# Giving each of five queues its own lead in a written-out instruction order: a four-layer graph network on one Trainium2 core

## The chip, the cores and the metric

The kernel runs as one program on one core of a Trainium2 chip. A core has five engines with a queue each: TensorE (PE) for matrix products, VectorE (DVE), ScalarE (ACT), GpSimd (POOL), and SyncE (SP), which only issues transfers. An engine works through its queue in order; between engines there are semaphores. The metric is the device time of one execution in microseconds (us), lower is better. The profile is one profiled execution of the same program.

## The reference

There are B = 32 independent batches of N = 512 nodes with D = 128 features, and a 512 x 512 adjacency matrix of zeros and ones with about 16 neighbours per node. Four layers follow one another, each as `x = x + layer(relu(layernorm(x)), adj)`:

```python
# layer 0: the largest value over the neighbours
p, q = h @ (W1 - W2), h @ W2
out = max over j of relu(p[i] + q[j] + b) * adj[i, j]
# layer 1: four steps, with earlier results concatenated (1, 1, 2, 3 inputs)
upd = concat(l2norm(adj, 2) @ (f @ ws + bs), f @ wn + bn, l2norm(adj, 1).T @ (f @ wd + bd))
f = tanh(upd @ wu + bu)
# layer 2
out = (adj / rowsum) @ (h @ weight) + bias
# layer 3: four steps of a gated recurrent unit
m = adj.T @ (h @ weight[i])
r, z = sigmoid(...), sigmoid(...); n = tanh(xn + r * hn); h = (1 - z) * n + z * h
```

All weights are shared by the batches.

## The kernel before, in words

`gnn_stack` calls `fast`, which computes all batches, then a flag that says whether any batch needs the slow path `general` (none does in these inputs). In `fast` a batch is 21 parts in a row:

- *prepare* (function `prepare`): load x and adj (1 MB, ACT's DMA queue), layer norm, transposes of adj (`pat`) into `at`, the products q and p (`pq`, then `qn`, `pn` on DVE), a table of q in DRAM (`qtab`, SP's queue).
- *counts*: prefix counts of each adjacency row as matmuls (`pc`), cast on ACT (`cc`) and spread by four SP transfers each (`ccd`).
- *keys*: degrees on POOL, the matmuls `pkey`, the largest eight of a row on DVE (`top`), from which indices of neighbours come (`idx`).
- *rows* and *gather0* to *gather3* (function `gathers`): 28 indirect transfers of table rows (`G`, POOL's queue), each taken into a running maximum `gm` on DVE; beside it one-hot matrices `oh` (DVE, some on ACT), matmuls `pa`, and their running maximum `acc` on DVE, 32 per batch, eight in each of the four gather parts.
- *first*: both maxima are joined to x1; adj is loaded again as `an` (POOL's queue).
- *layer1* and *layer10* to *layer13* (function `layer1`): each step transposes its input (`pf`), splits it into two fp32r parts (`hi` on ACT, `lo` on DVE), multiplies both by `at` and `an` (`pg`, 16 matmuls), scales on DVE (`ag`), and adds up `pu`; tanh on ACT gives `f`.
- *layer2*, *layer3* (function `layer23`): layer 2 and the norm before layer 3 (`po`, `pt`).
- *layer30* to *layer33*: a GRU step each: `pg` (8 matmuls), copy `mT`, the gate products `pk`, sigmoids on ACT (`gate`), `phn` and `pxn`, `nn` and `h` on DVE and POOL, transposes `ph`, and again `hi` and `lo`.
- *out*: the last sum `xo` and the store.

The order of each queue isn't that of the program text. Class `Flow` records every operation with an estimated duration (`cost`), up to AHEAD = 6 batches at a time, and gives them out one by one: in `step` it looks for the engine that can start something first, and on that engine, among the operations that can start at that time, takes the one with the smallest due time. The due time is set in `close`: the place of the batch times PACE, less the longest remaining chain inside the batch, less a lead of the part:

```python
op.due = n * self.pace - op.due - op.lead
```

Places come from `FIRST` and `LAST` (the first and last batches moved against an even spacing of one), and for the three groups of weight preparation from `WEIGHTS`: `first` (layer 0's weights), `rest` (layer 1's), `last` (layers 2 and 3). Leads come from function `lead`: `LEADS` for all batches, with `LEADS0` added for the first and `LEADSN` for the last. Before the change a part has one lead for all five queues, set as `F.lead` at the start of the part and copied to each operation in `note`. Where its own timeline leaves PE idle for over 1 us, `clock` puts in small matmuls with no use of their result (`spin`), so that PE's clock stays up. Transfers are recorded like other operations, on the queue of the engine that issues them.

The line 529 of the profile is the helper that issues nearly every instruction, so the profile is read by the names of tiles.

Of the kernel before, what the change touches and what calls it, by code (L numbers as in the profile page):

```python
# [32 lines left out]
CODES = ((0, 1), (P, 1), (2 * P, 2), (4 * P, 4))  # L33
ONACT = (2, 2, 1, 0)
NLEFT = 7
PACE = 46.14
SPACING = 1.5
AHEAD = 6
BANKS = (1, 2, 2, 1)

LEADS = {
    "prepare": -28.3, "counts": -7.5, "keys": 16.5, "rows": 26.6,
    "gather0": 59.4, "gather1": 70.0, "gather2": 28.0, "gather3": 53.5,
    "first": 61.2, "layer1": 43.0, "layer10": 30.3, "layer11": 8.7,
    "layer12": 56.0, "layer13": -41.3, "layer2": 39.7, "layer3": 5.5,
    "layer30": 99.5, "layer31": 189.8, "layer32": 213.5, "layer33": 84.7,
    "out": 56.0,
}

LEADS0 = {  # L50
    "prepare": 18.5, "counts": 53.1, "keys": 4.8, "rows": -15.7,
    "gather0": 52.2, "gather1": 93.4, "gather2": -34.5, "gather3": -69.1,
    "first": 0.5, "layer1": 141.7, "layer10": 10.1, "layer11": 110.3,
    "layer12": -73.8, "layer13": -13.4, "layer2": 6.9, "layer3": 56.5,
    "layer30": 35.3, "layer31": 29.8, "layer32": 117.9, "layer33": 64.0,
    "out": 75.9,
}
LEADSN = {
    "prepare": -19.9, "counts": -18.3, "keys": -42.0, "rows": 46.6,
    "gather0": 15.9, "gather1": -47.7, "gather2": -77.8, "gather3": -4.3,  # L60
    "first": 13.3, "layer1": -33.7, "layer10": 14.0, "layer11": -36.5,
    "layer12": 103.7, "layer13": 62.6, "layer2": 212.2, "layer3": 99.8,
    "layer30": 182.6, "layer31": 105.8, "layer32": 85.0, "layer33": 161.6,
    "out": -15.2,
}
FIRST = (1.57, 0.36, -0.05, 0.0)
LAST = (0.0, 0.18, 0.33, 0.24, 0.3)
WEIGHTS = (-3.98, -2.44, -5.94)

LATE = {  # L70
    "xn2": ("xn0", 1), "hi2": ("qn", 1), "lo2": ("gm", 1), "mT": ("acc", 1), "hg": ("hT0", 1),
# [29 lines left out]
class View:  # L101


    def __init__(self, tile, shape, dtype, steps=(), lanes=None, region=None):
        self.tile, self.shape, self.dtype = tile, tuple(shape), dtype
        self.steps, self.lanes, self.region = steps, lanes or (0, shape[0]), region
# [196 lines left out]
class Flow:  # L303
# [9 lines left out]
    SPIN, IDLE = 0.23, 1.0  # L313
    WINDOW = 3.413
    EVENT = 0.13
    ENGINES = ("pe", "vec", "act", "pool", "sync")

    def __init__(self, nc, pace, ahead, slack=0.0):
        self.nc, self.pace, self.ahead, self.slack = nc, pace, ahead, slack
        self.rings, self.part, self.lanes = {}, [], {}  # L320
        self.lead = 0.0
        self.free = dict.fromkeys(self.ENGINES, 0.0)
        self.busy = dict.fromkeys(self.ENGINES, 0.0)
        self.spin, self.window, self.active, self.rate = None, 0, 0.0, 1.0
        self.gathered, self.port, self.turn, self.queue = 0.0, 0.0, 0, {}
        self.seen = {e: {} for e in self.ENGINES}
        self.waiting = {e: [] for e in self.ENGINES}
        self.vec = Engine(self, "vec", nc.vector)
        self.act = Engine(self, "act", nc.scalar)
        self.pool = Engine(self, "pool", nc.gpsimd)  # L330
        self.sync = Engine(self, "sync", nc.sync)
# [49 lines left out]

    def note(self, engine, fn, args, kw, outs, ins, cost, after):
        op = Op(engine, fn, args, kw, cost, after)
        op.lead = self.lead
        seen = set()
        for writes, views in ((False, ins), (True, outs)):
            for v in views:
                if not isinstance(v, View):
                    continue
                buf = v.tile  # L390
                for u, seen_as, w in buf.uses:
                    if u is op or not (writes or w) or not v.meets(seen_as):
                        continue
                    if id(u) not in seen:
                        seen.add(id(u))
                        op.before.append(u)
                if writes and buf.real is None and buf not in op.new:
                    op.new.append(buf)
                if writes and v.region is None and v.lanes == (0, buf.rows):
                    buf.uses = [c for c in buf.uses if c[0] is op]  # L400
                buf.uses.append((op, v, writes))
                if buf not in op.bufs:
                    op.bufs.append(buf)
                    buf.left += 1
        self.part.append(op)
# [75 lines left out]
    def step(self):  # L481
        best = None
        for e in self.ENGINES:
            now = [(t, op) for op in self.waiting[e] if (t := self.start(op)) is not None]
# [20 lines left out]
        if op.engine == "pe":  # L505
            t = self.clock(op, t)
        cost = op.cost + (self.EVENT * max(0, len(need) - 1) if op.engine != "pe" else 0.0)
        if op.engine == "pe":
# [350 lines left out]
def fast(ctx: ExitStack, tc: tile.TileContext, a: dict, out: bass.AP, bad):  # L859
# [10 lines left out]

    F = Flow(nc, PACE, AHEAD)
    F.share(ps, 8, {f"ps{s}": n for s, n in enumerate(BANKS)} | {"idle": 0})

    def lead(b, stage):
        own = LEADS0 if b == 0 else LEADSN if b == B - 1 else {}
        return LEADS[stage] + own[stage] if stage in own else LEADS[stage]

    def bank(s, shape, dtype, name):
        return F.tile(ps, shape, dtype, f"ps{s}", name, BANKS[s])
# [13 lines left out]
    for i in range(2):  # L893
# [3 lines left out]
            out=t[2 * P :, :].rearrange("(k p) d -> p k d", p=P),  # L897
# [82 lines left out]
    def prepare(b, xt, af):  # L980
# [60 lines left out]
        for t, (first, step) in enumerate(CODES):  # L1041
            F.sync.dma_start(
                out=tab[first : first + (P - 1) * step + 1 : step, :], in_=qn[:, t, :]
            )
        F.lead = lead(b, "counts")


        ccd = []
        for jt in range(NT):
# [10 lines left out]
            ccd.append(d)  # L1060

        F.lead = lead(b, "keys")


# [48 lines left out]
    def gathers(b, at, ccd, qhl, pn, tab, idx, has, dinv):  # L1113
# [15 lines left out]
        for jt in range(NT):  # L1129
            F.lead = lead(b, f"gather{jt}")  # L1130
            for k in range(1, KSLOT + 1):
                oh = F.tile(big, [P, 2, N], F32R, tag="oh", name=f"oh_{b}_{jt}_{k}", bufs=3)
                if k > KSLOT - ONACT[min(b, len(ONACT) - 1)]:

                    far = F.tile(big, [P, 2, N], BF16, tag="far", name=f"far_{b}_{jt}_{k}")
                    F.act.activation(far, ccd[jt], AF.Abs, bias=W.slot[:, k : k + 1])
                    F.act.activation(oh, far, AF.Relu, bias=W.ones[:, 0:1], scale=-1.0)
                else:
                    F.vec.tensor_scalar(oh, ccd[jt], NBASE + k, None, ALU.is_equal)
                for u in range(2):  # L1140
                    pa = pst(3, f"pa_{b}_{k}_{jt}_{u}")
                    F.mm(flat(pa), qhl[:, jt, u, :], oh[:, u, :], start=True, stop=True)
                    if k == 1 and jt == 0 and u == 0:
                        F.act.copy(acc, flat(pa))
                    else:
                        F.vec.tensor_max(acc, acc, flat(pa))
# [212 lines left out]
    def spin(n):  # L1359
# [5 lines left out]
    places = [  # L1365
        b - FIRST[min(b, len(FIRST) - 1)] - LAST[max(0, b - B + len(LAST) - 1)] for b in range(B)
    ]
    F.run(
        list(zip(WEIGHTS, (W.first, W.rest, W.last)))
        + [(p, partial(batch, b)) for b, p in enumerate(places)]  # L1370
# [471 lines left out]
```

## Time and profile before

| | us |
|---|---|
| median of 3 runs | 2907.83 (2904.98 to 2911.66) |
| span of the profiled execution | 2909.0 |
| TensorE busy | 2795.8 |
| TensorE's weight loads (beside it) | 1794.6 |
| VectorE busy | 2299.1 |
| ScalarE busy | 1268.4 |
| GpSimd busy | 1848.5 |

For the profiled execution only its span is given, from the first to the last instruction. In the profile a group is named by what it writes and reads ("pg<-at,lo" is a matmul into pg from at and lo). "[0.90 <-DVE lo L529]" behind a line says that the engine was idle for 0.90 us before it and that DVE's lo ended that. A row that begins with two times and a colon gives the busy time of each engine in that stretch of the span, with the number of its instructions. The clock is that which the chip granted to TensorE, 1.00 being full.

### The profile page before, as it was taken

The page shows a single profiled execution, that of the slowest core. Times are in us where ns is not written, and L with a number is a line of the kernel's source. Part 1 is how long each engine was busy: PE and PEld are TensorE (multiplying, and loading weights), DVE is VectorE, ACT ScalarE, POOL GpSimd, SP SyncE. Part 2 cuts the span into 40 slices and gives each one's busy share as a digit, 9 for nine tenths or more (in the row PEclk, how much of TensorE's full clock was granted, in tenths as well). Part 3 has the DMA queues.
Part 4 walks back from the last instruction along what each step waited for, and adds up shares of the span by engine and source line. Part 5 has one row for each costly group of instructions (what it writes and reads, how often), then busy time and mean ns, then how long its engine had stood idle before and what let it go on. Part 6 is the DMA issues. An engine that isn't in the chain of part 4 may idle for free.

```text
span 2909.0 us, 38588 instructions
## 1 busy us (share of the span) xinstructions
PE 2795.8 (96%) x11766; PEld 1794.6 (62%) x11766; DVE 2299.1 (79%) x5371; ACT 1268.4 (44%) x2622; POOL 1848.5 (64%) x2020
## 2 busy tenths in 40 slices
PE   7799999999999999999999999999999999999998
PEld 4565566666666665666665666666666666566675
DVE  6778888788888888888788888888888888887634
ACT  6643344444444443444443444444444444443333
POOL 3666656666666766666766666776666666666522
PEclk9999999999999999999999999999999999999999
DMA  6644334323444433334423344433344433333200
GB/s 150 136 74 88 62 85 81 83 55 76 79 86 81 83 60 78 74 83 80 87 56 78 74 84 87 82 69 64 74 84 87 81 81 56 70 66 63 55 5 9
DMA packets 191270, 218.49 MB, mean 75 GB/s; under 512 B 30376, under 2 KB 139600, under 8 KB 191056
## 3 DMA queue, kind: packets, MB, share of 16 engines
q0 software_dynamic: 47104, 92.34, 23.1%
q1 hardware_dynamic: 73768, 63.63, 7.1%
q10 hardware_dynamic: 70184, 59.98, 6.8%
q8 instruction: 96, 1.57, 0.2%
q14 instruction: 118, 0.97, 0.1%
HBM read 164.32 MB, written 17.96 MB: 63 GB/s over the span
## 4 chain that ended last, share of the span: by engine, by line
PE 85%; DVE 7%; DMA 2%; issue 2%; ACT 2%; POOL 1%; SPq 0%; ACTq 0%; DVEq 0%; POOLq 0%
PE pg L529 26%; PE pu L529 19%; PE pk L529 14%; PE pa L529 7%; PE phn L529 4%; PE pxn L529 4%; DVE acc L529 3%; PE ph L529 2%; PE pq L529 2%; PE pkey L529 2%; PE pt L529 1%; DVE lo L529 1%; PE pf L529 1%; PE po L529 1%; PE px L529 1%
## 5 line engine op out<-in xcount | busy, mean ns | idle before, releaser
L529 POOL DMA_INDIRECT G<-qtab,idx x768 | 841.3, 1095 | 653.6 <-DVE gm L529 495.3
L529 DVE TENSOR_TENSOR acc<-acc,pa 128x512 f32<-128x512 f32 x992 | 673.4, 679 | 123.3 <-PE pa L529 97.6
L529 PE MATMUL pg<-an,lo 128*128 128x512 f32 (+1 forms) x1072 | 461.9, 433 | 0.0
L529 PE MATMUL pg<-an,hi 128*128 128x512 f32 (+1 forms) x1072 | 456.1, 428 | 4.8 <-PE spin L553 1.1
L529 PE MATMUL pa<-oh,qhl 128*128 128x512 f32 x1024 | 450.5, 508 | 6.1 <-DVE acc L529 2.1
L529 PE MATMUL pu<-ag,w 128*128 128x512 f32 (+1 forms) x952 | 448.0, 568 | 4.1 <-DVE ag L529 4.1
L529 DVE TENSOR_SCALAR oh<-ccd 128x1024 fp32r<-128x1024 bf16 x492 | 348.9, 723 | 62.4 <-PE pa L529 55.0
L529 ACT ACTIVATE xn<-x,shift,rstd 128x128 f32<-128x128 f32 x512 | 214.6, 483 | 261.4 <-POOL shift L529 255.7
L529 PE MATMUL pg<-at,lo 128*128 128x512 f32 (+1 forms) x672 | 295.9, 442 | 22.8 <-DVE lo L529 22.3
L529 PE MATMUL pg<-at,hi 128*128 128x512 f32 (+1 forms) x672 | 272.7, 407 | 8.4 <-ACT hi L529 7.2
L529 PEld LDWEIGHTS pa<-oh,qhl 128*128 128x128 f32 x1024 | 191.8, 193 | 135.5 <-issue 65.9
L529 PEld LDWEIGHTS pg<-an,hi 128*128 128x128 f32 x1072 | 202.6, 189 | 107.2 <-issue 62.5
L529 PEld LDWEIGHTS pg<-an,lo 128*128 128x128 f32 x1072 | 202.7, 189 | 85.9 <-issue 52.0
L529 PE MATMUL pk<-h,g_hh 128*128 128x512 f32 (+1 forms) x528 | 246.7, 582 | 1.2 <-DVE ag L529 1.1
L529 DVE TENSOR_TENSOR gm<-gm,G 128x128 f32<-128x128 f32 x768 | 242.4, 322 | 3.5 <-DMA G<-qtab,idx 3.3
L529 PE MATMUL pk<-mT,g_ih 128*128 128x512 f32 (+1 forms) x528 | 243.3, 580 | 0.5 <-ACT mT L529 0.5
L529 PEld LDWEIGHTS pu<-ag,w 128*128 128x128 f32 x952 | 177.0, 189 | 107.7 <-issue 80.3
L529 ACT ACTIVATE gate<-pk,bsum 128x512 f32<-128x512 f32 (+1 forms) x264 | 176.7, 672 | 151.3 <-PE pk L529 148.7
L529 DVE TENSOR_TENSOR ag<-pg,rbc 128x512 f32<-128x512 f32 (+1 forms) x272 | 172.5, 653 | 71.5 <-PE pg L529 69.7
L529 DVE SCALAR_TENSOR_TENSOR nn<-phn,bcol,gate 128x512 f32<-128x512 f32 (+1 forms) x132 | 96.3, 729 | 148.2 <-ACT gate L529 148.1
L529 ACT COPY mT<-pg 128x512 f32<-128x512 f32 (+1 forms) x164 | 94.3, 575 | 272.9 <-PE pg L529 265.4
L529 POOL TENSOR_TENSOR rstd<-rstd,mhalf 128x4 f32<-128x4 f32 x128 | 152.7, 1193 | 86.9 <-DVE shift L529 82.6
(178 smaller groups left out, 5146.7 us busy)
## 6 DMA issues: line engine op xcount, KB each, us to landing
af<-in_adj_dram ACTq DMA_DIRECT2D x32, 1024.0 KB
ccd<-cc SPq DMA_DIRECT2D x512, 64.0 KB
an<-in_adj_dram POOLq DMA_DIRECT2D x128, 256.0 KB, 3.4
x<-in_x_dram ACTq DMA_DIRECT2D x64, 256.0 KB
rbc<-scal SPq DMA_DIRECT2D x32, 512.0 KB
G<-qtab,idx POOLq DMA_INDIRECT x768, 3.9
qtab<-qn SPq DMA_DIRECT2D x128, 64.0 KB
out_dram<-xo ACTq DMA_DIRECT2D x32, 256.0 KB
```

The source lines that it names most:

```text
L529: op.fn(*(real(v) for v in op.args), **{k: real(v) for k, v in op.kw.items()})
```

## The change

Each entry of LEADS, LEADS0 and LEADSN becomes five numbers, one for each of the queues PE, VectorE, ScalarE, GpSimd and SyncE in this order, and `note` takes the one of the operation's queue. All numbers are new, those of PACE, FIRST, LAST and WEIGHTS too. The class value BEGIN gives the queues a start time of zero, as before. The operations, their data and their engines stay as they are.

```diff
-PACE = 46.14
+PACE = 47.946
...
 LEADS = {
-    "prepare": -28.3, "counts": -7.5, "keys": 16.5, "rows": 26.6,
-    "gather0": 59.4, "gather1": 70.0, "gather2": 28.0, "gather3": 53.5,
-    "first": 61.2, "layer1": 43.0, "layer10": 30.3, "layer11": 8.7,
-    "layer12": 56.0, "layer13": -41.3, "layer2": 39.7, "layer3": 5.5,
-    "layer30": 99.5, "layer31": 189.8, "layer32": 213.5, "layer33": 84.7,
-    "out": 56.0,
+    "prepare": (-96.3, 67.2, -62.6, -118.2, -54.6),
+    "counts": (-30.8, 75.5, 73.6, -63.8, 17.1),
+    "keys": (-34.9, 95.7, -16.3, -153.8, 2.8),
+    "rows": (-140.1, 135.8, -68.5, -113.3, 29.9),
+    "gather0": (55.9, 171.1, -70.3, 89.9, 66.1),
+    "gather1": (64.7, 170.3, 69.2, -121.6, 61.1),
+    "gather2": (-14.4, 101.9, 93.0, -89.5, 42.8),
+    "gather3": (-19.1, 173.6, -47.6, -14.1, 57.9),
+    "first": (14.8, 99.4, 60.7, -118.0, -22.6),
+    "layer1": (12.7, 222.4, 34.4, -13.6, 33.9),
+    "layer10": (-42.7, 277.2, -168.4, -48.9, 24.9),
+    "layer11": (-57.5, 67.9, -25.2, -56.5, -12.9),
+    "layer12": (18.9, 186.9, -22.9, -142.9, -19.8),
+    "layer13": (-146.8, 51.2, -134.2, -208.3, -59.5),
+    "layer2": (119.4, 329.2, 177.1, 141.4, 173.8),
+    "layer3": (-122.2, 42.5, -91.8, -231.4, -35.3),
+    "layer30": (42.5, 233.5, 4.3, 114.8, 93.2),
+    "layer31": (69.4, 279.5, 118.8, 121.5, 140.3),
+    "layer32": (367.7, 419.9, 353.4, 349.1, 343.5),
+    "layer33": (171.3, 369.4, 342.9, 136.5, 231.1),
+    "out": (-135.9, 190.4, 31.4, -177.9, -50.2),
 }
 LEADS0 = {
-    "prepare": 18.5, "counts": 53.1, "keys": 4.8, "rows": -15.7,
...
+    "prepare": (33.1, 91.4, 154.9, 212.2, 39.5),
+    "counts": (242.5, 316.5, 144.0, 245.1, 200.1),
...
 }
 LEADSN = {
-    "prepare": -19.9, "counts": -18.3, "keys": -42.0, "rows": 46.6,
...
+    "prepare": (-77.4, -195.4, -16.2, -139.8, 16.7),
+    "counts": (-25.7, 156.6, 149.6, -52.5, 83.0),
...
 }
-FIRST = (1.57, 0.36, -0.05, 0.0)
-LAST = (0.0, 0.18, 0.33, 0.24, 0.3)
-WEIGHTS = (-3.98, -2.44, -5.94)
+FIRST = (1.076, 0.113, 0.157, -0.873)
+LAST = (-0.429, -0.542, -0.763, 1.134, 0.230)
+WEIGHTS = (-3.94, -0.78, -5.78)
...
+    BEGIN = (0.0, 0.0, 0.0, 0.0, 0.0)
     ENGINES = ("pe", "vec", "act", "pool", "sync")
...
-        self.lead = 0.0
-        self.free = dict.fromkeys(self.ENGINES, 0.0)
+        self.lead = (0.0,) * 5
+        self.free = dict(zip(self.ENGINES, self.BEGIN))
...
-        op.lead = self.lead
+        op.lead = self.lead[self.ENGINES.index(engine)]
...
-        return LEADS[stage] + own[stage] if stage in own else LEADS[stage]
+        return tuple(map(sum, zip(LEADS[stage], own[stage]))) if stage in own else LEADS[stage]
```

The first entry of FIRST is batch 0's, and its last entry is that of batch 3 and of all later ones; the first entry of LAST is that of all batches up to the fifth from the end. A place is b - FIRST - LAST, so that a middle batch b had place b and has b + 1.302, and batch 0 goes from -1.57 to -0.647.

## The prediction

> **What bounds the kernel now.** I read the page first, then the waits of TensorE, then a table of 91 us stretches, then the timeline around the waits that come back in every batch. On the page:
>
> ```profile
> PE 2795.8 (96%) x11766; PEld 1794.6 (62%) x11766; DVE 2299.1 (79%) x5371; ACT 1268.4 (44%) x2622; POOL 1848.5 (64%) x2020
> PE   7799999999999999999999999999999999999998
> PE 85%; DVE 7%; DMA 2%; issue 2%; ACT 2%; POOL 1%; SPq 0%; ACTq 0%; DVEq 0%; POOLq 0%
> ```
>
> TensorE (PE) is busy for all but 113 us of the span, and the chain that ended last lies on it for 85%. The next engine, VectorE (DVE), has a fifth of its time free. A new order can give back only what PE stands still or spins (the 233 spin matmuls count as busy). Where that is, the stretches tell; columns are PE, weight loads, DVE, ACT, POOL, granted clock, DMA:
>
> ```profile
> 0.00:91.00 91.00, 66.22 (x365) 40.89 (x365) 57.24 (x145) 53.22 (x119) 41.43 (x80) 0.94 0.71 159
> 91.00:182.00 91.00, 75.73 (x412) 57.52 (x412) 69.16 (x181) 52.31 (x104) 57.27 (x65) 0.92 0.55 111
> 364.00:455.00 91.00, 86.19 (x359) 55.33 (x358) 75.08 (x181) 37.55 (x80) 54.12 (x59) 0.98 0.36 76
> 1001.00:1092.00 91.00, 89.36 (x393) 57.71 (x392) 75.19 (x179) 41.13 (x86) 62.07 (x70) 1.00 0.40 79
> 2821.00:2909.00 88.00, 74.50 (x340) 51.66 (x338) 36.58 (x93) 35.91 (x77) 25.21 (x32) 0.95 0.03 8
> ...
> 398.00:412.00 14.00, 10.31 (x34) 6.15 (x34) 11.36 (x22) 2.94 (x6) 6.71 (x6) 0.88 0.35 75
> ```
>
> The middle is full: 89.36 of 91 us at full clock, and DVE at 75.19. Against that level the first stretch lacks 23.1 us, the second 13.6, 364 to 455 3.2, the last 11.9. So there are three places: the start, the end, and 1.6 us in each stretch between.
>
> What repeats in the middle:
>
> ```profile
> 1031.61 0.81 PE L553 MATMUL spin<-code,identb 128*128 128x512 bf16 x3 [0.36 <-DVE lo L529]
> 1118.01 0.81 PE L553 MATMUL spin<-code,identb 128*128 128x512 bf16 x3 [0.36 <-DVE lo L529]
> ...
> 1073.18 0.58 ACT L529 CAST hi<-pf 128x512 fp32r<-128x512 f32 x1 [0.37 <-PE pf L529]
> 1073.58 1.46 DVE L529 TENSOR_TENSOR acc<-acc,pa 128x512 f32<-128x512 f32 x2
> 1074.96 0.68 DVE L529 TENSOR_TENSOR lo<-pf,hi 128x512 fp32r<-128x512 f32 x1
> 1075.70 0.50 PE L529 MATMUL pg<-at,lo 128*128 128x512 f32 x1 [0.90 <-DVE lo L529]
> ```
>
> The two spins are 86.40 us apart: that is the period of one batch, and the order in it repeats. In a period PE stands 0.90 us for a lo and 0.36 us before the spins. At the first place hi is ready at 1073.76, but DVE has two acc in front of lo. At the second lo starts as soon as hi is there, and PE has nothing else to do.
>
> **How full a period is.** From start to start in the timeline a 512-wide fp32r matmul takes 0.23 us, a 512-wide F32 one 0.858 (two records), a 128-wide F32 one 0.109, a bf16 one 0.056. A batch has 104 pg, 32 pa, 4 pc and 4 pu<-rows (144 x 0.23 = 33.1), 21 pu and 24 pk, phn and pxn (45 x 0.858 = 38.6), 57 of the third kind (6.2), 4 pq of 0.43 (1.7) and 48 bf16 ones (2.7): 82.3 us. Of the 4.1 us left, 2.2 are seen: 0.90 + 0.36, three spins of 0.216, and 0.3 until the next matmul. The rest are steps of under 0.25 us at changes of kind, which any order has.
>
> **The change part by part.** No operation and no byte is removed or added, only the order of each queue (and with it how many waits an instruction needs); the new class value BEGIN holds zeros, as the queues' start times did. Within a queue only differences of due times count, so a shift of a whole column does nothing (the DVE column of LEADS has mean 179, PE's 5).
>
> Leads by queue, middle batches. Less their column's mean, the new leads are wider: layer32 stood 163 us above the mean, and stands 241 (DVE) to 383 (POOL); layer33 went from 34 to between 167 and 312; layer11 from -42 to -111 on DVE. The last two GRU layers go first more often, so a batch is finished sooner, and layer1 of the next one is pushed back. About 26 periods run from the count matmuls of batch 4 (297 us) to those of batch 30 (2559 us). The period in the new order is not in the trace. Upper bound of gain: both waits and the spins go, 26 x 2.2 = 57 us. Bound of loss: one wait as long as the longest late one in the trace, 3.69 us at 404 us (PE for ag), in each period: 26 x 3.69 = +96. I take one of the two small waits gone, 26 x 0.9 = -23, as the place is DVE order alone (two acc of 0.73 us against a lo of 0.68) and a lead on DVE no longer drags PE's own order with it. Behind lo stand nn, acc and h; put back by 0.7 us they find cover, since DVE idles 15.0 us in a period (71.43 of 86.40 busy). If that cover is gone, each such step costs 0.7 us per batch.
>
> A row on gaps that grow: after the 3.69 us wait the stretch 398 to 412 us has a granted clock of 0.88, so 12% of 14 us, 1.7 us, are lost beside the wait. So a wait of this size costs 5.4 us, and one per period 26 x 5.4 = +140; that is the far end of the loss, and the 0.90 and 0.36 us waits show a clock of 1.00. [...]
>
> The start: FIRST, LEADS0 and WEIGHTS. By the place lists, batch 0 stood 72 us ahead of the middle batches' spacing and stands 93; batch 1 goes from 17 to 47, batch 2 from 2 behind to 49 ahead. The weights of layer 1 ("rest") were due 40 us before batch 0 and are now 6 us before it. Their DMAs (SP and ACT queues) and copies on ACT move behind batch 0's casts and one-hot steps; the qtab and ccd issues on SP, about 2.4 us for four ccd, move with them. Of the 36.7 us missing up to 182 us, four waits hold 17.5: 4.27 (constants), 4.60 (xn of the first load), 3.96 and 4.63 (loads of layer 3's weights). The first two no order removes. Bounds: all but those two and half of the rest saved, -14; a load of "rest" that comes late, as the 17.2 us that ACT waited once for wn, +17. I take 0 up to 182 us, because the matmuls that move ("rest") lie in gaps that pa leaves while it waits for DVE's acc and oh, 57 and 69 us busy in these stretches; if those gaps close, the 14 us of spare bound are what is at stake. After 182 us I take the one wait at 404 us as gone with its clock loss, -5.
>
> The end: LAST and LEADSN. Batch 30 goes from 11 us ahead to 75, batch 31 from 14 to 32, batch 29 from 15 ahead to 16 behind. The last stretch lacks 11.9 us, all in the chain of batch 31's GRU layers (hi, lo, nn, h of 0.4 to 0.7 us each), which nothing else covers once batch 30 is out. With batch 30 earlier there is less beside it. Bounds -8 and +20 (the 11.9 again and half as much); I take 0, the middle being held by the same chain.
>
> PACE, 46.14 to 47.946: distances between batches grow by 3.9%, 1.8 us for neighbours, small beside the leads. I give it nothing; bound 0.36 us, the smaller repeating wait, per period, +-9.
>
> Sum: 2909.0 - 23 - 5 = 2881 against the profiled execution. Its span is 1.2 us over the median of the runs (2907.83), inside their spread, so I take it as that: 2880.
>
> **The rivals.**
>
> 1. Only the start gains (or the end). The middle is full, and a new order turns the same pattern with the same two small waits. For it: 89.36 us in stretch after stretch. Against: the period depends on which lo meets which acc, and that is chosen anew. Time 2908 - 5 to -14: 2898.
>
> 2. Nothing measurable: gains at one place are paid at another, 2902 to 2914. A measurement of this kernel can tell about 0.2%, 6 us, from no change.
>
> 3. Slower by lo on DVE. At 1074.31 DVE chose an acc of the last gather part (gather3) over the lo of layer11. Gather3's lead was 44.8 us above layer11's; on DVE it is now 105.7 above, so acc goes ahead by 61 us more. If two more acc stand in front, lo and PE's pg come 2 x 0.73 = 1.46 us later in each period: 26 x 1.46 = +38, 2946; one more, +19, 2927. It decides from 28 / 26 = 1.1 us a period, one and a half acc more. Against it: hi itself may now come when no acc is ready, and a PE with other batches' work waits for nothing.
>
> 4. Slower by the end: the chain of batch 31 alone, with batch 30 done early, +10 to +20: 2923.
>
> **How the numbers follow.** Forecast (period shorter by 0.4 to 2 us, own range 2856 to 2895): 0.42. Rival 1: 0.19. Rival 2: 0.07. Rival 3: 0.23. Rival 4: 0.09. Faster is 0.42 + 0.19 = 0.61, the same 0.07, slower 0.32. Below 2853 I leave 0.08 (all of 57 us in the middle would be 2851), above 2942 0.1, the upper half of rival 3 and all with a clock that falls. The range is 2853 to 2942.
>
> **What would show it.** The period: spins or count matmuls of neighbours in the middle 85.0 to 85.8 us apart, instead of 86.40; the wait of pg for DVE lo, 22.3 us in 25 cases, under 10, and the clock 1.00 in all middle stretches. The stretch 364 to 455 us fuller by 3 us. The last 88 us at 74 us of PE, as before. I am wrong if the period is above 86.4 (rival 3: the lines of waits for DVE lo or acc grow), or if the period falls and the span doesn't: then the start or the end took it, and the count matmuls of batch 4 come later than 297 us or more than 272 us lie behind those of batch 31 (2637 us).

## The result: slower by 1.6%

| | before | after |
|---|---|---|
| median, us | 2909.74 (4 runs) | 2957.02 (4 runs) |
| ratio | | 1.0162, interval 1.0146 to 1.0178 |
| span of the profiled execution, us | 2909.0 | 2948.1 |

The profiled execution of after is the fastest of its four runs (2949.85), so its trace explains 39 us of a loss of 47. The first lines of the page of after, with PE's and VectorE's (DVE) slices and the chain that ended last:

```profile
PE 2791.6 (95%) x11693; PEld 1787.2 (61%) x11709; DVE 2443.6 (83%) x5371; ACT 1271.8 (43%) x2622; POOL 1854.9 (63%) x2020
PE   7899999999999999999999999999999999999998
DVE  6877898888898888888788988888898888888634
PE 72%; DVE 15%; issue 6%; DMA 4%; ACT 1%; POOL 1%; SPq 0%; DVEq 0%; ACTq 0%; POOLq 0%
```

PE is 4 us less busy than before; DVE is 144.5 us busier with the same 5371 instructions, and its share of the chain went from 7% to 15%. The three groups of DVE that grew, of after and then of before (mean ns of one behind the busy time):

```profile
L575 DVE TENSOR_SCALAR oh<-ccd 128x1024 fp32r<-128x1024 bf16 x492 | 438.6, 910 | 10.0 <-PE pa L575 9.0 <-DMA ccd<-cc 0.9
L575 DVE TENSOR_TENSOR gm<-gm,G 128x128 f32<-128x128 f32 x768 | 269.6, 358 | 21.4 <-DMA G<-qtab,idx 21.0
L575 DVE TENSOR_TENSOR nn<-nn,zc 128x512 f32<-128x512 f32 x132 | 132.9, 1007 | 8.2 <-ACT nn L575 7.2 <-POOL zc L575 1.0
```

```profile
L529 DVE TENSOR_SCALAR oh<-ccd 128x1024 fp32r<-128x1024 bf16 x492 | 348.9, 723 | 62.4 <-PE pa L529 55.0 <-DMA ccd<-cc 7.3
L529 DVE TENSOR_TENSOR gm<-gm,G 128x128 f32<-128x128 f32 x768 | 242.4, 322 | 3.5 <-DMA G<-qtab,idx 3.3
L529 DVE TENSOR_TENSOR nn<-nn,zc 128x512 f32<-128x512 f32 x132 | 109.7, 832 | 7.7 <-ACT nn L529 6.0 <-POOL zc L529 1.6
```

oh, gm and nn took 89.7, 27.2 and 23.2 us more, 140 of the 144.5. acc, as large as nn and 992 times there, stayed at a mean of 679 ns, and none of the 992 took over 691. A difference between them: acc reads one of its inputs from PSUM, gm and nn read both from SBUF. oh has a single tensor as input, also in SBUF, so two inputs aren't what all three share.

Where the 39 us lie follows from the starts of the count matmuls pc. Batch 4's are at 295.1 us (296.8 before), batch 30's at 2600.5 (2558.5), batch 31's at 2682.9 (2637.4). So the start gave 1.7 us, the 26 periods took 2305.4 instead of 2261.7 us (43.7 more, 88.7 instead of 87.0 each), the next period took 3.5 more, and the end gave 6.4: 39.1 in all. The waits of PE over the span of after:

```profile
PE ph L575 <- DVE h L575: 46.6, 56, 1.7
PE pu L575 <- DVE acc L575: 31.2, 24, 1.3
PE pg L575 <- ACT hi L575: 11.3, 26, 0.4
```

Before, ph waited 4.6 us for h, and pg 22.3 us for DVE's lo; the latter is down to 0.2. A period of after has three larger waits for DVE. All three have the same picture ahead of them. The timeline of after around them (the lines of DVE, GpSimd and PE that matter):

```profile
1115.51 0.99 POOL L575 DMA_INDIRECT G<-qtab,idx  x1 [0.17 <-DVE nn L575]
1115.96 2.43 DVE L575 TENSOR_SCALAR oh<-ccd 128x1024 fp32r<-128x1024 bf16 x1
1116.54 1.29 POOL L575 TENSOR_TENSOR gate<-h,gate 128x512 f32<-128x512 f32 x1
1118.31 0.68 DVE L575 TENSOR_TENSOR nn<-nn,zc 128x512 f32<-128x512 f32 x1
1120.29 0.68 DVE L575 TENSOR_TENSOR h<-gate,nn 128x512 f32<-128x512 f32 x1
1121.03 0.66 PE L575 MATMUL ph<-ident,h 128*128 128x128 f32 x4 [0.79 <-DVE h L575]
...
1148.45 1.00 POOL L575 DMA_INDIRECT G<-qtab,idx  x1 [0.17 <-DVE nn L575]
1148.92 2.02 DVE L575 TENSOR_TENSOR gm<-gm,G 128x128 f32<-128x128 f32 x1
1149.48 1.30 POOL L575 TENSOR_TENSOR gate<-h,gate 128x512 f32<-128x512 f32 x1
1152.67 0.69 DVE L575 TENSOR_TENSOR h<-gate,nn 128x512 f32<-128x512 f32 x1
1153.51 0.63 PE L575 MATMUL ph<-ident,h 128*128 128x128 f32 x4 [0.98 <-DVE h L575]
...
1165.62 2.29 DVE L575 TENSOR_TENSOR nn<-nn,zc 128x512 f32<-128x512 f32 x1
1166.05 1.30 POOL L575 TENSOR_TENSOR gate<-h,gate 128x512 f32<-128x512 f32 x1
1167.83 0.67 DVE L575 TENSOR_TENSOR acc<-acc,pa 128x512 f32<-128x512 f32 x1
1168.56 0.50 PE L575 MATMUL pu<-rows,b8r 128*128 128x512 f32 x1 [1.29 <-DVE acc L575]
```

The gm of 0.28 us takes 2.02 and ends at 1150.94, 0.16 us after GpSimd's product z * h ("gate<-h,gate") ends; the oh of 0.69 takes 2.43 and ends 0.56 us after the product's end. Each stands in DVE's queue ahead of an nn and an h, and PE's ph waits for h. At 1165.62 an nn of 0.68 takes 2.29 us beside a third product, and PE's pu waits 1.29 us for the acc behind it.

To see how much of DVE's time this is, take every DVE instruction that lies more than 0.25 us over the median of its group and shape, add up what it lies over, and note which GpSimd operation (transfers left out) overlaps it most. Below, this sum is called the stretch. Before: 72 us, of them 49 beside z * h. After: 210 us; 140 beside z * h (29 gm, 28 oh and 32 nn, 1.42 to 1.67 us each), 26 beside gm<-gm,pn (23 oh), 40 beside lo<-xn,hi. The expectations below go by a count that is a little lower: 71 before, 198, 137 and 56 (the last for gm and lo together) after.

The GpSimd transfer ahead of the product isn't what holds DVE: in after 101 gm begin during the issue of a G that no GpSimd operation follows within 0.2 us, and none takes more than 0.29 us; the 27 that begin during one with z * h right behind take 2.01 in the median.

That is the theory to be tested, A: GpSimd's wide two-input products hold up DVE instructions, and the new order puts more of them side by side. The rival, B: the order puts h and acc too late on DVE, whatever GpSimd does.

### The profile page after: what moved, and what is told of

Read it like the earlier page. It is cut to its first block, busy times and chain, and to the rows that moved or that the text cites. A ratio compares the mean times of both kernels' runs of the same rounds, so it can differ in the third digit from the quotient of the medians.

```text
span 2948.1 us, 38419 instructions
## 1 busy us (share of the span) xinstructions
PE 2791.6 (95%) x11693; PEld 1787.2 (61%) x11709; DVE 2443.6 (83%) x5371; ACT 1271.8 (43%) x2622; POOL 1854.9 (63%) x2020
## 4 chain that ended last, share of the span: by engine, by line
PE 72%; DVE 15%; issue 6%; DMA 4%; ACT 1%; POOL 1%; SPq 0%; DVEq 0%; ACTq 0%; POOLq 0%
PE pu L575 19%; PE pg L575 18%; PE pk L575 14%; PE pa L575 4%; DVE acc L575 4%; PE phn L575 4%; DVE nn L575 3%; PE pxn L575 3%; PE ph L575 2%; DVE gm L575 2%; PE pq L575 2%; DMA G<-qtab,idx 2%; PE pkey L575 1%; DVE h L575 1%; DVE st L575 1%
## 5 line engine op out<-in xcount | busy, mean ns | idle before, releaser
L575 PE MATMUL pg<-an,hi 128*128 128x512 f32 (+1 forms) x1072 | 463.8, 434 | 0.8 <-ACT hi L575 0.2
L575 PE MATMUL pg<-an,lo 128*128 128x512 f32 (+1 forms) x1072 | 450.9, 422 | 0.0
L575 DVE TENSOR_SCALAR oh<-ccd 128x1024 fp32r<-128x1024 bf16 x492 | 438.6, 910 | 10.0 <-PE pa L575 9.0
L575 PE MATMUL pa<-oh,qhl 128*128 128x512 f32 x1024 | 432.6, 488 | 5.4 <-DVE top L575 1.6
L575 PE MATMUL pg<-at,lo 128*128 128x512 f32 (+1 forms) x672 | 310.5, 463 | 3.0 <-POOL lo L575 2.8
L575 DVE TENSOR_TENSOR gm<-gm,G 128x128 f32<-128x128 f32 x768 | 269.6, 358 | 21.4 <-DMA G<-qtab,idx 21.0
L575 ACT ACTIVATE at<-pat 128x512 fp32r<-128x512 bf16 x128 | 75.5, 595 | 238.4 <-PE pg L575 181.6
```

The lines of the kernel that those rows point to most:

```text
L575: op.fn(*(real(v) for v in op.args), **{k: real(v) for k, v in op.kw.items()})
```

## The experiments

**The product z * h without its second input, in the changed kernel.** The order is computed from the same estimates, so it is that of after; only what is issued differs, and the product h * z is left out of the result. `a_gate1`, in the class that records operations:

```diff
-            self.flow.note(self.name, fn, args, kw, outs, ins, cost, after)
+            did = self.swap(op, fn, outs)
+            self.flow.note(self.name, did, args, kw, outs, ins, cost, after)
...
+        if self.name != "pool" or op not in ("tensor_mul",) or outs[0].free_size() < 256:
+            return fn
+        f = self.real.tensor_scalar
...
+        def one(out, a, b):
+            for _ in range(2):
+                f(out, b, 1.0, 0.0, ALU.mult, ALU.add)
...
```

> The changed kernel in the same written-out order, but GpSimd's product z * h (gate<-h,gate, two inputs, 1.27 us) is issued as two scalings of z alone by 1.0 (one input, about 0.64 us each by the row of zc); so h * z is left out of the result. Theory A (GpSimd's two-input products hold up VectorE instructions that run beside them): the 137 us by which oh, gm and nn lie over their medians beside gate go, VectorE's busy time falls from 2443.6 to about 2305, the waits of ph for h (46.6) and of pu for acc (31.2) nearly vanish, the period falls from 88.5 to about 85.5 us and the time from 2957 to about 2880 (2860 to 2900). Theory B (the order itself puts h and acc too late on VectorE, whatever GpSimd does): busy time and waits as before, 2950 to 2960.

Measured: 2862.69 us, ratio to the kernel before 0.9836 (0.9819 to 0.9852), 94 us less than after, and inside the range. The two traces have the same 5371 DVE instructions in the same order. The stretch beside gate fell from 140 to 28 us, and PE's waits of ph for h from 46.6 to 2.0, of pu for acc from 31.2 to 0.6. GpSimd's group and DVE's oh and gm in a_gate1:

```profile
L356 POOL TENSOR_SCALAR gate<-gate 128x512 f32<-128x512 f32 (+1 forms) x264 | 182.1, 690 | 16.3
L588 DVE TENSOR_SCALAR oh<-ccd 128x1024 fp32r<-128x1024 bf16 x492 | 406.3, 845 | 8.3 <-PE pa L588 7.2 <-DMA ccd<-cc 1.1
L588 DVE TENSOR_TENSOR gm<-gm,G 128x128 f32<-128x128 f32 x768 | 236.7, 315 | 26.0 <-DMA G<-qtab,idx 24.2 <-issue 1.4
```

GpSimd spent 182.1 us on it instead of 167.3, so it isn't a shorter GpSimd that helps. Theory B falls: with DVE's order untouched the waits are gone. Batches 4 to 30 now take 85.3 us each. DVE's busy time missed its forecast (2354.3 us instead of about 2305): beside a one-input scaling a DVE instruction still took 0.3 to 0.4 us more, and the two-input operations gm<-gm,pn and lo<-xn,hi are left as they were.

**All wide two-input operations of GpSimd, the same way.** `a_all1` is a_gate1 with `("tensor_mul", "tensor_sub", "tensor_add")`.

> As a_gate1, and also the other wide two-input operations of GpSimd (lo<-xn,hi, gm<-gm,pn, x<-gm,x, x<-x,b) as two one-input scalings each; these sums and differences are left out of the result. Theory A: the other 56 us of stretched oh and gm go too, VectorE busy about 2250, period 84.5 to 85.2, time 2840 to 2870. Theory B: 2950 to 2960. If only gate matters: equal to a_gate1.

Measured: 2851.41 us, ratio 0.9801 (0.9784 to 0.9817). oh fell to a mean of 756 ns; the time is inside its range, but only another 11 us are gone. DVE's busy time is 2305.0 us where about 2250 was expected: beside the scalings it took 0.3 to 0.5 us more at a time (some 60 us in all). The gate product was most of it.

**The same in the kernel before.** `b_gate1` is the edit of a_gate1 on the old order.

> The kernel before in its own order, with gate<-h,gate as two one-input scalings, h * z left out of the result. Theory A: the gm that took 1.32 us at 1072.34 beside gate takes 0.28, acc and lo come 1 us earlier, PE's wait of 0.90 us in each period goes: 26 x 0.9, 2908 to about 2885 (2880 to 2892), period 85.5. Theory B: 2905 to 2912, period 86.4.

Measured: 2882.26 us, ratio 0.9910 (0.9893 to 0.9928). Most periods are 85.7 us, and the wait of pg for lo is 10.2 us instead of 22.3: halved, not gone. So the same thing cost the old order some 27 us, and with this one product out of the way the new order (2862.69) is 20 us ahead of the old one. Both of these kernels leave h * z out; no run takes the other products out of the old order.

**Four pieces, every result kept.** `a_split` and `b_split` issue each wide two-input operation of GpSimd as four, on the new and on the old order:

```diff
...
+        def four(out, a, b):
+            for t in range(out.shape[1]):
+                f(out[:, t, :], a[:, t, :], b[:, t, :])
...
```

> The changed kernel in the same order, every result kept, with each wide two-input operation of GpSimd issued as four of a quarter's width. Theory A, if VectorE gets in between two pieces: a stretched instruction waits for 0.3 to 0.5 us instead of 1.3 to 1.7, the stretched total falls from 198 to under 80 us, time 2880 to 2910. Theory A, if GpSimd's pieces follow each other without a gap for VectorE: 2955 to 2975, as the pieces take longer together. Theory B: 2950 to 2960.

> The kernel before in its own order, every result kept, with each wide two-input operation of GpSimd issued as four of a quarter's width, as a_split did with the changed kernel (2957 to 2918.7, stretch 198 to 64 us). Theory A: the 71 us of stretch fall to 25 to 40, PE's 0.90 us wait gets shorter, and GpSimd is some 200 us busier with nothing waiting for it: 2885 to 2900, faster than the kernel before. If GpSimd's longer operations come back as waits (lo, x): 2905 to 2925.

Measured: a_split 2918.74 us (1.0032, 1.0021 to 1.0043), b_split 2914.41 us (1.0021, 1.0010 to 1.0031). The cut gives the new order 38 us back; its stretch fell to 77 us, as the first expectation had it, but the time lies 9 us above its range. On the old order the stretch fell from 72 to 62 us only, and something is paid elsewhere: the second expectation. A quarter costs 0.49 to 0.50 us in b_split, four of them 2 us instead of 1.3, and what waits for them shows up (b_split's waits):

```profile
PE ph L542 <- DVE h L542: 19.9, 34, 3.0
...
DVE h L542 <- POOL gate L311: 20.0, 19, 2.5
```

**Four pieces for the gate product alone.** `b_gsplit` and `a_gsplit`:

> As b_split, but the gate product alone is issued as four. Theory A: of the 71 us, 49 lie beside gate and fall to about 15; lo and x keep their length, so nothing that waits for them is later: 2883 to 2897, as b_gate1 (2882) or a little over. If GpSimd's longer gate is what counts: 2905 to 2920.

> The changed kernel in its own order, every result kept, with the gate product alone on GpSimd issued as four of a quarter's width, as b_gsplit did with the kernel before (2910 to 2894). Theory A: the 137 us of stretch beside gate fall to about 40, those beside lo and gm (56) stay; the period falls from 88.5 to 85.3 to 86, time 2880 to 2900, so that the new order is at least as good as the old one (2894) once the gate product is cut. If the cut costs GpSimd (b_split, 2914) as much as it saves: 2910 to 2925, as a_split (2918.7).

Measured: b_gsplit 2893.86 us, ratio 0.9942 (0.9922 to 0.9962); a_gsplit 2905.80 us, ratio 0.9995 (0.9981 to 1.0008). b_gsplit computes everything and is faster than both kernels, 0.6% below before and 2.1% below after. The time is in the range, but not for the reason given in full: the stretch beside gate fell from 49 to 33 us where 15 was expected, and with what grew elsewhere it is 70 us in all, as before. What went is the part of gm (27 us to 3), and gm stands ahead of lo. PE waits 9.0 us for lo instead of 22.3:

```profile
PE pg L542 <- DVE lo L542: 9.0, 23, 1.2
```

a_gsplit missed its range by 6 us. Its stretch fell to 90 us, 32 of them beside gate (40 expected), but the gate product is now 2.1 us long, and two new waits stand in each period, which the profile of a_gsplit shows:

```profile
PE pg L588 <- DVE lo L588: 22.7, 25, 0.9
PE pk L588 <- ACT mT L588: 14.6, 24, 0.7
```

So, with every result kept, the cut takes 51 us off after and brings it level with the kernel before: the whole loss of 47 is back. But the old order gains from the same cut too and is then 12 us ahead of the new one. The lead of 20 us that a_gate1 showed can't be had this way.

**Two halves.** `b_ghalf` cuts the gate product of the old order once.

> The kernel before, with the gate product in two halves. A quarter took 0.51 us, so four take 0.8 us more than the 1.27 us of one; a half should take 0.7. Theory A: VectorE is held for at most a half; time 2888 to 2900, within 6 us of b_gsplit. If both halves hold VectorE as one piece: 2905 to 2912.

Measured: 2924.70 us, ratio 1.0045 (1.0031 to 1.0059), a miss, slower than uncut. Beside gate 27 gm lie 1.16 us each over their median, as uncut (1.05): DVE didn't get in between two halves of 0.82 us, and both together are longer than the whole was (1.64 against 1.33). The wait for lo is 22.5 us, as in the kernel before. That explains why nothing is won. The 15 us lost go with the clock: its five runs have a mean granted clock of 0.985 to 0.991, the slowest (2931.52) the lowest and the fastest (2916.11) the highest, where the kernel before has 0.992 to 0.994; 0.006 of 2909 us are 17, an estimate.

**A small operation ahead of the product.** In the trace of after 27 gm and 26 oh started about 0.55 and 0.53 us before a gate product that follows a G issue, and 24 nn 0.43 us before one that follows an issue of an; all of them ended 0.16 us (gm) or 0.56 us (oh, nn) after the product's end. In the kernel before, 24 oh that started 0.33 us ahead of a product following zc weren't held, and the product took 1.62 us instead of 1.30. That gave theory C: behind a transfer issue the product holds DVE already before its own recorded start. `a_sep` puts a small scaling between the two, where `self.issuing` says that the last operation on GpSimd was a transfer:

```diff
+        if op.wide and self.issuing:
+            self.between()
...
+    F.between = lambda: nc.gpsimd.tensor_scalar(gap, W.mhalf[:, 0:4], 1.0, 0.0, ALU.mult, ALU.add)
```

`a_sepm` has `nc.gpsimd.memset(gap, 0.0)` there, `b_sep` is a_sep's edit on the old order.

> The changed kernel in the same order, every result kept, with one small one-input GpSimd operation (a scaling of 128x4, about 0.27 us) issued in front of each wide two-input operation that directly follows a DMA issue on GpSimd. In the changed kernel's trace VectorE's gm, oh and nn that started 0.43 to 0.56 us before a gate product that follows a DMA issue ended 0.16 to 0.56 us after its end, while those before a product that follows zc weren't held. Theory C (behind a DMA issue the product holds VectorE up already from before its recorded start): the small operation stands in that place, VectorE's instruction gets through first, the stretched total falls from 198 us to under 100, time 2870 to 2900. Theory A without C (any overlap costs, whatever stands in front): 2950 to 2965, a little slower for about 100 x 0.27 us on GpSimd. Theory B: 2955 to 2965.

> As a_sep, with a memset of 128x4 (no input) as the small operation. Theory C with any operation that isn't a DMA issue: equal to a_sep within 8 us. If it takes an operation that reads: 2940 to 2965.

> The kernel before in its own order, with the same small scaling in front of wide two-input operations that follow a DMA issue. Theory C: gm beside gate (27 of its 71 us of stretch) falls, PE's wait of 0.90 us in each period goes: 2885 (2880 to 2895). Theory A without C: 2905 to 2915.

Measured: a_sep 2914.87 us (1.0026, 1.0014 to 1.0037), a_sepm 2960.31 us (1.0176, 1.0153 to 1.0199), b_sep 2941.68 us (1.0118, 1.0101 to 1.0135). The three don't agree with C, and a_sep and b_sep lie outside all their ranges. a_sep gained 42 us and nearly lost the gm beside gate (48 us to 4), but its stretch is 172 us in all, not under 100: 21 oh that started 0.69 us ahead of the product, before the small operation too, were still held until 0.56 us after its end. The memset changed nothing (stretch 216 us). On the old order the same edit made the gm beside gate worse (27 to 40 us), and b_sep's clock is 0.983 to 0.986 instead of 0.991 to 0.994, by an estimate some 20 of its 32 us. What the small operation did, as I read it, is to move GpSimd by 0.2 us here and there; which DVE instruction then meets a product is another matter each time. C isn't shown.

**The ends alone.** `ends_new` has the old LEADS and PACE, each lead the same on all five queues, and the new LEADS0, LEADSN, FIRST, LAST and WEIGHTS.

> Old LEADS and PACE for the middle, the new LEADS0, LEADSN, FIRST, LAST and WEIGHTS: the change's ends alone. If the parts of the change add up, the period stays at 86.4 us and the time is 2895 to 2915. If the order of the middle is one whole with its start (any number changed gives another order): a period that doesn't settle, 2960 to 3050.

Measured: one run of 3018.68 us beside 2909.2 for the kernel before. Its periods lie between 71 and 132 us from the third to the tenth and don't settle after that up to batch 30 (82.9 to 103.0). DVE's stretch is 109 us, about half of after's, and PE spins and waits instead. So at least these parts of the change can't be added up: with the old leads and the old PACE in the middle, another start gave another order of the middle too.

## Why the prediction was wrong

**The bound.** PE full in the middle, the chain on PE, three places to gain: read rightly, and the place where the time moved was the middle. Yet the page's share of DVE (79%) was taken as room, and it was the engine that mattered.

**Leads by queue, middle batches.** This is the step that failed: it has -23 us, the trace has +43.7 for the 26 periods. It took the lengths of DVE's instructions as fixed and only their order as new, so it had no term for what GpSimd does to them. It took the 0.90 us wait for a matter of DVE's order alone, two acc ahead of a lo. Ahead of those two acc in the same timeline of before, not read then, stands a gm beside a gate product:

```profile
1072.17 1.33 POOL L529 TENSOR_TENSOR gate<-h,gate 128x512 f32<-128x512 f32 x1
1072.34 1.32 DVE L529 TENSOR_TENSOR gm<-gm,G 128x128 f32<-128x128 f32 x1
```

b_gate1 shows that this product made up over half of lo's lateness (22.3 to 10.2 us); the rest is left with the product out of the way. The wait itself did go in after, as forecast (22.3 to 0.2 us), and so did the spins of the middle (81 between 278 and 2579 us before, one after). Three other waits took their place, 1.29, 0.98 and 0.79 us, all behind stretched instructions. Nor did the 15.0 us that DVE idles in a period give the cover that the step counted on: h and acc came late at the places where PE had nothing else.

**The bounds of that step** (a gain of 57, a loss of 96) held. The three new waits sum to 3.1 us per period, against the 2.2 that went with the old waits and the spins: 0.9 net, 23 us in 26 periods. With the clock, below, that is some 32 of the 43.7; the rest isn't traced to a place.

**The clock.** The prediction had it at 1.00 in all middle stretches, and lost only beside a wait of 3.69 us. In after seven of the 91 us stretches between 364 and 2548 us stand at 0.98, two in before; for the same 91 us, after and then before:

```profile
1183.00:1274.00 91.00, 87.47 (x353) 55.14 (x354) 78.69 (x173) 39.17 (x82) 58.93 (x67) 0.98 0.38 75
1183.00:1274.00 91.00, 89.37 (x369) 56.88 (x368) 75.12 (x174) 40.45 (x85) 60.63 (x65) 1.00 0.41 87
```

At 2% of 91 us each, the five more are an estimated 9 of the 43.7 us. In this stretch the clock is 0.50 from 1257.0 to 1260.4 us, just after the 1.29 us wait of pu that ends at 1256.4. So here the clock fell behind a wait much shorter than the 3.69 us of the prediction's row. Of the 24 waits of pu for acc in the middle of after (1.28 to 1.33 us) six have such a fall right behind them and 18 have none; nor has either of two waits of 2.14 us, at 664.6 and 930.6 us. In before the clock fell once behind the wait of pg for lo, 0.89 us long (0.50 from 1162.9 to 1166.3 us). Why it fell behind these waits and not behind the others isn't shown, and no run shows what the spins do for it.

**The start.** Given 0 up to 182 us and -5 after it, got 1.7 us by batch 4's count matmuls: the direction right. In the first 91 us PE is 2.3 us fuller (68.54), in the second 3.4 (79.13):

```profile
0.00:91.00 91.00, 68.54 (x358) 42.32 (x361) 60.87 (x153) 57.30 (x126) 43.26 (x81) 0.87 0.69 164
91.00:182.00 91.00, 79.13 (x454) 61.59 (x460) 74.65 (x202) 54.08 (x103) 61.55 (x69) 0.94 0.55 114
```

Against it the clock fell from 0.94 to 0.87 in the first stretch.

**The end.** Given 0 within -8 and +20; 265.2 us lie behind batch 31's count matmuls instead of 271.6, so -6.4, inside the bounds. Rival 4, slower by the end, is out.

**PACE.** Not tried alone.

**Rival 3** had the sign and nearly the size (2946 for two more acc; 2957), but not the mechanism, so its size is luck. It had lo of layer11 kept back by acc of gather3; the wait of pg for lo went, and those of ph for h and of pu for acc grew.

**The chances.** Slower had 0.32 and the range ended at 2942. A term for GpSimd beside DVE would have widened it: of the 72 us of stretch before, 58 lie in the 26 middle periods, 2.2 each, and a new order deals them anew; after has 7.5 each. The kernel's text points at this term: class `Engine` sets `port` on every VectorE tensor_scalar and on VectorE and GpSimd operations with two wide inputs in SBUF, and `start` lets none of these begin, in the planner's timeline, before the last one given out has ended.

**What the product holds up.** Beside z * h a gm takes 2.02 us instead of 0.28. Acc, with an input from PSUM, wasn't held: in before 26 acc that start 0.46 us (median) ahead of a product behind an issue of an take 0.67 to 0.69 us each; in after 24 nn that start 0.43 us ahead of such a product take 2.27 to 2.31. Beside a one-input scaling, which reads SBUF too, gm wasn't held to the end: the 27 gm of a_gate1 that begin ahead of one take 0.65 us and end 0.53 us before it does. By the records gm starts 0.56 us ahead of the product and waits all the same, as far as the records of GpSimd can be trusted. What sets this apart inside the chip, no run shows.

## What to carry to other kernels

A written-out order is only as good as the times in its timeline. In the middle of after the planner put in no spin between 278 and 2578 us, so its own timeline saw no gap of PE worth one, and on the chip 3 us of waits stood in each period. The rule that keeps gm, oh and nn apart from GpSimd's product is in the planner (`port`), and on the chip they met in nearly every period (29 gm, 28 oh and 32 nn were held beside it in after): what is kept apart only by estimated times, and not by a semaphore, can meet. When one engine's instructions get longer with the same count, look for a second engine's instruction that ends just before they do, ahead of any reading of priorities. To test it, keep the order and change only what the suspect reads.

## What the runs showed that I had not expected

- A VectorE instruction can be held from before the recorded start of GpSimd's product, 0.43 to 0.69 us in after and a_sep. Why isn't settled: the record of GpSimd's spans may be rough, or the product may hold DVE while the issue ahead of it still runs. The issue alone doesn't (gm at most 0.29 us). A product made to wait for the VectorE instruction by a semaphore wasn't tried.
- Cutting the GpSimd product in four cost it 0.8 us (0.51 us a quarter against 1.27) and let VectorE in (the stretch of gm beside gate from 27 us to 3 in b_gsplit); cutting it in two cost 0.3 and didn't (27 gm still 1.16 us each over their median in b_ghalf).
- Small shifts count for more than the edit: one operation of 0.21 us (the median in a_sep) ahead of some GpSimd products gave 42 us on one order and took 32 on the other, the clock's share included.
